# The last stage of a gated two-block transformer: extremes beside GpSimd's power, the clip factor inside the maxima's product, late products kept in PSUM, the last tokens in halves

## The chip, the cores and the metric

The kernel runs on one core of one Trainium2 chip. A core has five engines with queues of their own: TensorE (PE: matrix products into PSUM), VectorE (DVE), ScalarE (ACT), GpSimd (POOL) and SyncE (SP), which here only issues transfers between the chip's memory and SBUF. An engine works through its queue in order and waits on semaphores that other engines raise. The metric is the device time of one execution in microseconds (us); three runs of the kernel before took 977.98, 979.28 and 980.5, a median of 979.28. All times below are in us unless ns is written, and stand from the start of the profiled execution's span.

## The reference, cut to what matters

Eight batches of 256 tokens with 256 features pass four gated residual blocks: a cross attention with 16 heads, a slot router, a second cross attention with 8 heads of 128, and a feed-forward block (FFN) with simulated int8 quantization. The change is in the last of these and in the norm ahead of it:

```python
def _act_fake_quant(x, clip_factor):
    scale = jax.nn.sigmoid(clip_factor) * jnp.max(jnp.abs(x)) / QMAX
    return jnp.clip(_ste_round(x / scale), -QMAX - 1.0, QMAX) * scale
...
xq = _act_fake_quant(x, clip_x[0])
gate = jnp.einsum('bsh,ih->bsi', xq, _weight_fake_quant(w_gate))
up = jnp.einsum('bsh,ih->bsi', xq, _weight_fake_quant(w_up))
h = _act_fake_quant(jax.nn.silu(gate) * up, clip_down[0])
return jnp.einsum('bsi,hi->bsh', h, _weight_fake_quant(w_down))
...
x = x + jnp.tanh(g_ffn[1]) * _L1_ffn_ref(_layernorm(x, axis=-1), ...)
```

The two maxima run over all tokens of all batches, so nothing of the FFN can begin before the last batch's norm is known, and nothing of its second product before the largest h is known.

## The kernel before, in words

Tokens lie 128 to a tile of partitions, so a batch is two halves (t = 0, 1) of 128 x 256. All batches' x stay in SBUF (`xs`), and their normalised, transposed form for the FFN goes into `cs`.

**The second attention and what runs beside it.** `attention1` walks over 8 batches x 8 heads. For each head TensorE makes keys (L1081), scores (L1124), transposes of the exponentials (L1138) and sums (L1152); VectorE takes the scores' maxima (L1125) and ScalarE the exponentials (L1126). Every second head brings queries (L1045, moved to SBUF by VectorE at L1054), and after the eighth head the projection follows (L1165, added to x at L1179). The first attention and the router run as small pieces in between; their last pieces, of the last batches, end with `hn` (L893), `svo` (L924) and `scatter` (products L930, added to x at L932). When they are drained, at the first head of the last batch, `ffn_weights` is called: it opens the pool `fw` for the FFN's weights and, behind it, a staging pool `fs`. Both take over memory of the first block's pools, and every first use of a buffer waits for the last use of what lay there. Two staging buffers `wup` take the gate and up weights by SP's transfers (L1239, L1243) and `wdn` the down weights (L1276). VectorE reduces each to its scales (L1228) and quantizes it (L1221), ScalarE casts (L1222). The scheduler mixes these with the attention's instructions in VectorE's queue.

**The last norm.** For the last batch `norm` takes mean and variance (`ln_stats`: L251, L252), adds epsilon (L254), and GpSimd takes the power -1/2 (L255). Since the maximum of |x| after the norm follows from the extremes before it, VectorE takes maximum and minimum of each half (L1190) and puts them through the norm (L1192); the normalisation itself (L260, into `xl`) is kept back as `late`.

**The scale.** `act_scale` reduces the maxima per partition (L1467), and TensorE multiplies that column, spread over 128 columns, with the identity (L1472), which brings every partition all 128 values; VectorE takes their maximum (L1475), multiplies by the clip factor and 1/127 (L1477) and takes the reciprocal (L1479). Behind L1472, TensorE runs filler products (`keep_busy`, L1348; 8 after the first scale, 9 after the second). It is called for x, with `late` between the reduction and the product, and for h.

**The FFN.** x is quantized (L1487 on ScalarE, L1489 on VectorE), for the later batches by GpSimd's converting transfers (L1491); `expand` multiplies by the gate and up weights (L1512), ScalarE takes the silu (L1520) and partly the second factor (L1524), VectorE (L1527) or GpSimd (L1525) the product. After the scale of h it is quantized (L1581, L1582) with ScalarE and VectorE taking turns by a table, and for each batch TensorE makes two times six products of 128 x 256 into one PSUM bank (L1616). VectorE multiplies by the row of scales into `y` in SBUF (L1626), GpSimd (batches 0 to 3) or VectorE (4 to 7) adds x (L1630), SP sends the batch out (L1631). The last batch goes in two halves of tokens; in VectorE's queue both its products stand ahead of both its sums.

Of the kernel before, what the change touches and what calls it, by code (L numbers as in the profile page):

```python
# [9 lines left out]
F32 = mybir.dt.float32  # L10
# [6 lines left out]
ALU = mybir.AluOpType  # L17
AX = mybir.AxisListType
# [3 lines left out]
P = 128  # L22
B, S, D = 8, 256, 256
EPS = 1e-5
# [16 lines left out]
QMAX = 127.0  # L41
# [59 lines left out]
def flamingo_kernel(ctx: ExitStack, tc: tile.TileContext, a: dict, out: bass.AP):  # L101
    nc = tc.nc
    V, A, G, T = nc.vector, nc.scalar, nc.gpsimd, nc.tensor
# [16 lines left out]
    xs, cs = [], []  # L120
# [70 lines left out]
    ident = keep.tile([P, P], F32, tag="ident", name="ident")  # L191
# [49 lines left out]
    amax = keep.tile([P, B + 3], F32, tag="amax", name="amax")  # L241


    powers = []

    def ln_stats(src, name):

        st = small.tile([P, 2, 6], F32, tag=f"st{name}", name="st")
        mv = small.tile([P, 2, 2], F32, tag=f"mv{name}", name="mv")
        for i in range(2):  # L250
            V.bn_stats(st[:, i, :], src[:, i, :])  # L251
            V.bn_aggr(mv[:, i, :], st[:, i, :])  # L252
        rstd = small.tile([P, 2], F32, tag=f"rs{name}", name="rstd")
        V.tensor_scalar(rstd, mv[:, :, 1], EPS, None, ALU.add)  # L254
        powers.append(G.tensor_tensor(rstd, rstd, mhalf, ALU.pow).ins)  # L255
        return mv, rstd

# [747 lines left out]
    class Batch1:  # L1005
# [175 lines left out]
        def norm(self):  # L1181
            b = self.b
            self.xl = at1.tile([P, 2, D], F32, tag="tn", name="xl") if b < B - 1 else ffn["xl"]
            mv, rstd = ln_stats(xs[b], "e")
            if b == B - 1:

                ends = amax[:, b:].rearrange("p (t i) -> p t i", t=2)
                for i, op in enumerate((ALU.max, ALU.min)):
                    for t in range(2):
                        V.tensor_reduce(ends[:, t, i : i + 1], xs[b][:, t, :], AX.X, op)  # L1190
                for t in range(2):
                    V.tensor_scalar(  # L1192
                        ends[:, t, :], ends[:, t, :], mv[:, t, 0:1], rstd[:, t : t + 1], ALU.subtract, ALU.mult
                    )
                self.late = lambda: ln_apply(self.xl, xs[b], mv, rstd)
                return
            ln_apply(self.xl, xs[b], mv, rstd)
            V.tensor_reduce(amax[:, b : b + 1], self.xl, AX.XY, ALU.max, apply_absolute_value=True)
# [5 lines left out]
    def ffn_weights():  # L1204
# [129 lines left out]
            turns.append(late)  # L1334

        ffn["turns"] = [go for pair in zip(*turns[:2]) for go in pair] + turns[2]
        ffn["xl"] = fw.tile([P, 2, D], F32, tag="xl", name="xl")
        ffn.update(hq=hq, wg_s=wg_s, wu_s=wu_s, wgT=wgT, wuT=wuT, wdT=wdT, wd_row=wd_row)
        side.add([(0.7, go) for go in work])

    ffn = {}
# [111 lines left out]
    with (  # L1453
# [10 lines left out]
        def act_scale(maxima, clip_col, name, after, between=None):  # L1464

            m = fk.tile([P, 2], F32, tag=f"m{name}", name=f"m{name}")
            V.tensor_reduce(m[:, 0:1], maxima, AX.X, ALU.max, apply_absolute_value=True)  # L1467
            if between:
                between()

            pt = one()
            rows = T.matmul(pt[:, :P], m[:, 0:1].to_broadcast([P, P]), ident, start=True, stop=True)  # L1472
            with tc.issue_after(rows.ins):
                keep_busy(one(), after)
            V.tensor_reduce(m[:, 1:2], pt[:, :P], AX.X, ALU.max)  # L1475
            s = fk.tile([P, 1], F32, tag=f"s{name}", name=f"s{name}")
            V.tensor_scalar(s, m[:, 1:2], clip_col, 1.0 / QMAX, ALU.mult, ALU.mult)  # L1477
            r = fk.tile([P, 1], F32, tag=f"r{name}", name=f"r{name}")
            V.reciprocal(r, s)  # L1479
            return s, r  # L1480

        def quantize(engines, dst, src, r, name):
# [9 lines left out]
            else:  # L1492
                return (A.copy if to_bf16 == "A" else V.tensor_copy)(dst, q).ins

        sx, rx = act_scale(amax, clip[:, 0:1], "x", WARM[1], final.late)
        A.copy(cs[B - 1], turned_in(one(), final.xl))
        xqT = fk.tile([P, 2, B * S], BF16, tag="xqT", name="xqT")
# [113 lines left out]

        for b in range(B):
            pd = one().rearrange("p (t d) -> p t d", t=2)
            for t in range(2):
                for i in range(IC):
                    T.matmul(  # L1616
                        pd[:, t, :],
                        hq[:, b, i, t * P : (t + 1) * P],
                        wdT[:, i, :],
                        start=i == 0,  # L1620
                        stop=i == IC - 1,
                    )
            y = fp.tile([P, 2, D], F32, tag="y", name="y", bufs=B)
            for at in (slice(0, 2),) if b < B - 1 else (slice(0, 1), slice(1, 2)):
                n = at.stop - at.start
                V.tensor_tensor(  # L1626
                    y[:, at, :], pd[:, at, :], srow[:, None, :].to_broadcast([P, n, D]), ALU.mult
                )
                add = G if b < B // 2 else V
                add.tensor_tensor(y[:, at, :], y[:, at, :], xs[b][:, at, :], ALU.add)  # L1630
                nc.sync.dma_start(out=out_v[b][:, at, :], in_=y[:, at, :])  # L1631


# [39 lines left out]
```

## Time and profile before

| | |
|---|---|
| median of 3 runs | 979.28 (977.98 to 980.5) |
| the profiled execution | 977.07 |
| its span, from first to last instruction | 975.2, 13331 instructions, granted clock 0.996 |

How the engines' time is spread (busy time in us, share of the span, instructions):

```profile
PE 937.1 (96%) x4875; PEld 692.3 (71%) x4877; DVE 618.5 (63%) x1622; ACT 466.0 (48%) x922; POOL 139.9 (14%) x181
```

And by stretches of the end (each line: the stretch, its length, then busy time and instructions of PE, PEld, DVE, ACT, POOL, the granted clock, the DMA engines' busy share, GB/s):

```profile
880.00:919.00 39.00, 38.97 (x180) 28.86 (x179) 16.63 (x35) 16.92 (x37) 0.98 (x2) 1.00 0.00 1
919.00:928.00 9.00, 7.69 (x41) 5.06 (x39) 4.81 (x18) 0.86 (x2) 1.68 (x3) 1.00 0.00 1
...
932.00:952.00 20.00, 19.48 (x88) 8.51 (x88) 17.17 (x16) 20.00 (x36) 17.70 (x16) 1.00 0.20 35
952.00:959.00 7.00, 5.22 (x26) 2.37 (x24) 6.22 (x12) 2.00 (x4) 1.27 (x1) 1.00 0.00 0
959.00:970.00 11.00, 10.74 (x98) 9.29 (x95) 9.58 (x15) 6.89 (x5) 4.96 (x4) 1.00 0.33 112
970.00:975.20 5.20, 0.00 (x0) 0.00 (x0) 2.05 (x6) 0.00 (x0) 0.00 (x0) 0.81 0.51 172
```

The attention ends near 919, the last norm and the first scale take until 928, the expansion until 952, the second scale until 959, the last products until 970, and the last sums and transfers until 975. Filler products count as TensorE's busy time, so its busy share says little between 923 and 959.

### The profile page before, as it was taken

What the parts mean: (1) busy time and instruction counts of PE and PEld (TensorE: products, weight loads), DVE (VectorE), ACT (ScalarE), POOL (GpSimd) and SP (SyncE); (2) the same over time, 40 slices, a digit from 0 to 9 for tenths busy, and PEclk for the clock granted to TensorE, in tenths of its full rate; (3) what the DMA queues carried; (4) which work ended last, traced back from release to release, by engine and by line L of the source; (5) the groups of instructions that cost most, each with busy time, mean ns of one, the idle gap of its engine ahead of it and who ended that gap; (6) DMA issues with size and microseconds to landing.
All of it is one profiled execution on the core that took longest, in us unless ns stands there. A gap on an engine that the chain in (4) does not pass through costs nothing.

```text
span 975.2 us, 13331 instructions
## 1 busy us (share of the span) xinstructions
PE 937.1 (96%) x4875; PEld 692.3 (71%) x4877; DVE 618.5 (63%) x1622; ACT 466.0 (48%) x922; POOL 139.9 (14%) x181
## 2 busy tenths in 40 slices
PE   4989999999999999999999999999999999999996
PEld 3767778887777777777777677676667776777744
DVE  8765777774656747665657655566865365364487
ACT  3786545553546434554544443543434334333494
POOL 7101210110110202101011000013100010000172
PEclk9999999999999999999999999999999999999999
DMA  6803201111211102120001000000200000000012
GB/s 148 249 2 94 81 22 44 57 52 44 74 36 44 45 2 64 44 65 23 22 23 44 23 23 22 1 1 4 87 1 1 1 1 0 1 1 1 1 33 87
DMA packets 35186, 38.13 MB, mean 39 GB/s; under 512 B 10480, under 2 KB 30640, under 8 KB 35120
## 3 DMA queue, kind: packets, MB, share of 16 engines
q1 hardware_dynamic: 33488, 36.48, 12.8%
q0 software_dynamic: 1632, 0.79, 0.5%
q8 instruction: 39, 0.64, 0.3%
q14 instruction: 27, 0.22, 0.1%
HBM read 28.08 MB, written 8.39 MB: 37 GB/s over the span
## 4 chain that ended last, share of the span: by engine, by line
PE 82%; DVE 9%; ACT 5%; DMA 1%; issue 1%; POOL 1%; SPq 1%; DVEq 0%; ACTq 0%; POOLq 0%
PE bank_m L1152 10%; PE bank_m L1101 10%; PE bank_m L1081 10%; PE bank_m L1124 9%; PE bank_m L1045 5%; PE bank_m L1138 5%; PE bank_m L1165 5%; PE bank_z L623 3%; PE bank_z L649 2%; PE bank_z L531 2%; PE bank_z L660 2%; PE bank_s L876 1%; PE bank_z L703 1%; PE bank_z L560 1%; PE bank_z L272 1%
## 5 line engine op out<-in xcount | busy, mean ns | idle before, releaser
L1126 ACT ACTIVATE e<-bank_m,nm 128x512 f32<-128x512 f32 x128 | 88.0, 688 | 143.7 <-DVE nm L1125 141.6
L1152 PE MATMUL bank_m<-eT,v 128*128 128x256 f32 x496 | 120.6, 381 | 1.1 <-ACT k L1088 0.8
L1081 PE MATMUL bank_m<-kvT,w1kv 128*128 128x512 f32 (+1 forms) x256 | 118.4, 575 | 0.8 <-ACT e L1126 0.8
L1152 PEld LDWEIGHTS bank_m<-eT,v 128*128 128x128 f32 x496 | 92.4, 190 | 32.4 <-issue 14.8
L1101 PE MATMUL bank_m<-w1kv,kvT 128*128 128x256 f32 x480 | 110.0, 379 | 0.0
L1124 PE MATMUL bank_m<-k,q 128*128 128x512 f32 x224 | 109.5, 594 | 0.0
L1125 DVE TENSOR_REDUCE nm<-bank_m 128x1 f32<-128x512 f32 x128 | 87.6, 687 | 27.4 <-PE bank_m L1124 23.6
L1101 PEld LDWEIGHTS bank_m<-w1kv,kvT 128*128 128x128 f32 x480 | 89.8, 190 | 11.5
L652 ACT ACTIVATE e<-bank_z 128x512 f32<-128x512 f32 x112 | 62.8, 597 | 73.3 <-PE bank_z L649 72.9
L1054 DVE TENSOR_SCALAR q<-bank_m,bq 128x256 f32<-128x256 f32 x64 | 27.9, 477 | 87.3 <-PE bank_m L1045 87.3
L255 POOL TENSOR_TENSOR rstd<-rstd,mhalf 128x2 f32<-128x2 f32 x48 | 35.4, 741 | 322.7 <-DVE rstd L254 273.5
L626 DVE TENSOR_REDUCE nf<-bank_z 128x2 f32<-128x512 f32 x112 | 74.3, 681 | 9.7 <-PE bank_z L623 9.2
L1108 DVE COPY v<-bank_m 128x512 f32<-128x512 f32 x62 | 42.5, 686 | 55.2 <-PE bank_m L1101 55.2
L1138 PEld LDWEIGHTS bank_m<-ident,e 128*128 128x128 f32 x512 | 59.7, 141 | 23.6 <-issue 16.5
L1138 PE MATMUL bank_m<-ident,e 128*128 128x128 f32 x512 | 71.7, 274 | 1.3 <-DVE q L1054 1.0
L1159 ACT ACTIVATE oT<-bank_m,bv 128x256 f32<-128x256 f32 x64 | 30.3, 474 | 80.9 <-PE bank_m L1152 80.9
L1088 ACT ACTIVATE k<-bank_m,bk 128x512 f32<-128x512 f32 (+1 forms) x64 | 42.4, 662 | 47.5 <-PE bank_m L1081 47.1
L1045 PE MATMUL bank_m<-kvT,w1q 128*128 128x256 f32 x256 | 62.7, 381 | 1.7 <-DVE kvT L1035 1.4
L1128 DVE TENSOR_SCALAR e<-e,rs 128x512 f32<-128x512 f32 x128 | 62.1, 485 | 2.2
L1081 PEld LDWEIGHTS bank_m<-kvT,w1kv 128*128 128x128 f32 x256 | 43.3, 190 | 26.3 <-issue 22.1
L1165 PE MATMUL bank_m<-w1o,oT 128*128 128x256 f32 x256 | 60.1, 380 | 0.2 <-DVE x L1179 0.2
L1045 PEld LDWEIGHTS bank_m<-kvT,w1q 128*128 128x128 f32 x256 | 47.9, 190 | 11.0 <-DVE kvT L1035 2.2
(383 smaller groups left out, 1613.6 us busy)
## 6 DMA issues: line engine op xcount, KB each, us to landing
qs<-dqb SPq DMA_DIRECT2D x96, 64.0 KB, 2.6
ks<-dkb SPq DMA_DIRECT2D x48, 128.0 KB, 2.7
c<-in_ctx_dram SPq DMA_DIRECT2D x8, 256.0 KB, 3.3
x<-in_x_dram SPq DMA_DIRECT2D x8, 256.0 KB, 3.1
w1kv<-in_L_xattn_Wkv_dram SPq DMA_DIRECT2D x4, 512.0 KB, 5.4
out_dram<-y SPq DMA_DIRECT2D x7, 256.0 KB, 3.1
dqb<-hi SPq DMA_DIRECT2D x6, 256.0 KB, 2.2
dqb<-lo SPq DMA_DIRECT2D x6, 256.0 KB, 2.2
```

What stands on the lines that cost most here:

```text
L626: V.tensor_reduce(full[:, 2 * half : 2 * half + 2], ps, AX.X, ALU.max, negate=True)
L652: A.activation(e[:, i, :, :], ps, AF.Exp)
L1045: T.matmul(pq[:, i, :], w1q[:, c, h * P : (h + 1) * P], self.kvT[:, c, S:], start=c == 0, stop=c == 1,)
L1081: T.matmul(pk[:, at], w1kv[:, c, h * P : (h + 1) * P], self.kvT[:, c, at], start=c == 0, stop=c == 1,)
L1101: T.matmul(pv[:, k, :], (self.mT, self.kvT[:, :, S:])[half][:, c, k * P : (k + 1) * P], w1kv[:, c, at : at + 2 * P], start=c == 0, stop=c ...
L1124: T.matmul(ps, q, self.k[h], start=True, stop=True)
L1125: V.tensor_reduce(nm[:, at], ps, AX.X, ALU.max, negate=True)
L1126: A.activation(e[:, qc, :], ps, AF.Exp, bias=nm[:, at], accum_out=sums[:, at])
L1128: V.tensor_scalar(e[:, qc, :], e[:, qc, :], rs[:, at], None, ALU.mult)
L1138: T.transpose(pt[:, k, qc * P : (qc + 1) * P], self.e[h][:, qc, kc * P : (kc + 1) * P], ident)
L1152: T.matmul(po, self.v[h // 2][kc // 2][:, kc % 2, (h % 2) * P : (h % 2 + 1) * P], self.eT[:, kc, :], start=kc == 0, stop=kc == 3,)
L1165: self.projected = T.matmul(self.pp[:, qc, :], self.oT[:, h, qc * P : (qc + 1) * P], w1o[:, h, :], start=h == 0, stop=h == H1 - 1,).ins
```

## The change: what it does

Four edits of the last stage:

- The last norm's extremes are taken half by half, those of the second half behind the addition of epsilon in VectorE's queue, that is beside GpSimd's power; mean and reciprocal deviation are then applied to all four extremes by two operations with broadcast operands, in place of one operation for each half.
- Two diagonal matrices `dx` and `dh` (identity x clip factor / 127) are made in `ffn_weights` and kept in the pool `fw`. TensorE multiplies the maxima by them in place of the identity, and the scaling at L1477 goes. `late` is issued behind the reduction of the maxima.
- For batches 4 to 7 the product with the row of scales is written back to PSUM in place of SBUF, and the sum reads it there.
- The second half of the last batch's tokens is multiplied, scaled, added and sent in two pieces of 128 features.

```diff
-        V.tensor_scalar(rstd, mv[:, :, 1], EPS, None, ALU.add)
+        ready_for_power.append(V.tensor_scalar(rstd, mv[:, :, 1], EPS, None, ALU.add).ins)
...
-                for i, op in enumerate((ALU.max, ALU.min)):
-                    for t in range(2):
-                        V.tensor_reduce(ends[:, t, i : i + 1], xs[b][:, t, :], AX.X, op)
                 for t in range(2):
-                    V.tensor_scalar(
-                        ends[:, t, :], ends[:, t, :], mv[:, t, 0:1], rstd[:, t : t + 1], ALU.subtract, ALU.mult
-                    )
+                    with ExitStack() as late:
+                        if t:
+
+                            late.enter_context(tc.issue_after(ready_for_power[-1]))
+                        for i, op in enumerate((ALU.max, ALU.min)):
+                            V.tensor_reduce(ends[:, t, i : i + 1], xs[b][:, t, :], AX.X, op)
+                V.tensor_tensor(ends, ends, mv[:, :, 0:1].to_broadcast([P, 2, 2]), ALU.subtract)
+                V.tensor_tensor(ends, ends, rstd[:, :, None].to_broadcast([P, 2, 2]), ALU.mult)
...
+        ffn["scaled"] = {}
+        for i, name in enumerate("xh"):
+            at = ffn["scaled"][name] = fw.tile([P, P], F32, tag=f"d{name}", name=f"d{name}")
+            V.tensor_scalar(at, ident, clip[:, i : i + 1], 1.0 / QMAX, ALU.mult, ALU.mult)
         ffn["xl"] = fw.tile([P, 2, D], F32, tag="xl", name="xl")
...
-            V.tensor_reduce(m[:, 0:1], maxima, AX.X, ALU.max, apply_absolute_value=True)
+            found = V.tensor_reduce(m[:, 0:1], maxima, AX.X, ALU.max, apply_absolute_value=True).ins
             if between:
-                between()
+                with tc.issue_after(found):
+                    between()
...
-            rows = T.matmul(pt[:, :P], m[:, 0:1].to_broadcast([P, P]), ident, start=True, stop=True)
+            rows = T.matmul(pt[:, :P], m[:, 0:1].to_broadcast([P, P]), scaled[name], start=True, stop=True)
...
-            s = fk.tile([P, 1], F32, tag=f"s{name}", name=f"s{name}")
-            V.tensor_scalar(s, m[:, 1:2], clip_col, 1.0 / QMAX, ALU.mult, ALU.mult)
+            s = m[:, 1:2]
...
-            for t in range(2):
+
+            whole = [(t, slice(0, D)) for t in range(2)]
+            parts = whole if b < B - 1 else whole[:1] + [(1, slice(d, d + P)) for d in (0, P)]
+            for t, d in parts:
                 for i in range(IC):
                     T.matmul(
-                        pd[:, t, :],
+                        pd[:, t, d],
                         hq[:, b, i, t * P : (t + 1) * P],
-                        wdT[:, i, :],
+                        wdT[:, i, d],
...
-            for at in (slice(0, 2),) if b < B - 1 else (slice(0, 1), slice(1, 2)):
+            for at, d in ((slice(0, 2), slice(0, D)),) if b < B - 1 else [(slice(t, t + 1), d) for t, d in parts]:
                 n = at.stop - at.start
-                V.tensor_tensor(
-                    y[:, at, :], pd[:, at, :], srow[:, None, :].to_broadcast([P, n, D]), ALU.mult
-                )
-                add = G if b < B // 2 else V
-                add.tensor_tensor(y[:, at, :], y[:, at, :], xs[b][:, at, :], ALU.add)
-                nc.sync.dma_start(out=out_v[b][:, at, :], in_=y[:, at, :])
+                scale = srow[:, None, d].to_broadcast([P, n, d.stop - d.start])
+                add, to = (G, y) if b < B // 2 else (V, pd)
+                V.tensor_tensor(to[:, at, d], pd[:, at, d], scale, ALU.mult)
+                add.tensor_tensor(y[:, at, d], to[:, at, d], xs[b][:, at, d], ALU.add)
+                nc.sync.dma_start(out=out_v[b][:, at, d], in_=y[:, at, d])
```

More of the change, by code (lines that the diff above doesn't have):

```diff
@@ L241, in flamingo_kernel @@
     amax = keep.tile([P, B + 3], F32, tag="amax", name="amax")
-    powers = []
+    powers, ready_for_power = [], []
     def ln_stats(src, name):
@@ L1493, in quantize @@
                 return (A.copy if to_bf16 == "A" else V.tensor_copy)(dst, q).ins
+        scaled = ffn["scaled"]
         sx, rx = act_scale(amax, clip[:, 0:1], "x", WARM[1], final.late)
```

## The prediction

> **What bounds the kernel now.** I read the page's chain of work first, then the chain in order of time over the end of the run, then the waits of one window where TensorE is not full.
>
> ```profile
> PE 82%; DVE 9%; ACT 5%; DMA 1%; issue 1%; POOL 1%; SPq 1%; DVEq 0%; ACTq 0%; POOLq 0%
> ```
>
> TensorE is the bound for most of the span, so what lies beside it is free there. The edited places are three stretches in which it waits. The first is the last norm and the scale of x. Columns: start, length, what (all in us from the span's start):
>
> ```profile
> 923.56 0.48 DVE x L1179
> 924.04 0.04 DVE offset L1574
> 924.08 0.43 DVE st L251
> 924.50 0.32 DVE amax L1190
> 924.82 0.09 DVE mv L252
> 924.91 0.30 DVE amax L1190
> 925.22 0.09 DVE rstd L254
> ...
> 925.44 0.70 POOL rstd L255
> 926.14 0.03 issue
> 926.16 0.48 DVE amax L1192 x2
> 926.64 0.32 DVE xl L260
> 926.96 0.09 DVE mx L1467
> 927.04 0.14 issue
> 927.18 0.46 PE big L1472 x2
> ```
>
> Everything is serial here: two extremes stand in front of the power, one normalisation of x (L260) in front of the reduction that TensorE awaits. The second is the end, on VectorE:
>
> ```profile
> 965.85 0.69 DVE L1626 TENSOR_TENSOR y<-big,srow 128x512 f32<-128x512 f32 x1 [0.62 <-PE big L1616]
> 966.57 1.53 DVE L1630 TENSOR_TENSOR y<-y,x 128x512 f32<-128x512 f32 x1
> 968.02 0.68 DVE L1626 TENSOR_TENSOR y<-big,srow 128x512 f32<-128x512 f32 x1
> ```
>
> The sum of batch 4 takes 1.53 where the same form has a median of 0.692; a GpSimd sum of two SBUF tiles runs from 966.29 to 967.55 beside it. The products, with one operand in PSUM, run beside such GpSimd sums at 0.69. The third lies 280 us earlier, where the FFN's weights are loaded and quantized (columns: who waited for what, us in total, times, longest):
>
> ```profile
> PE bank_m L1138 <- DVE q L1054: 1.0, 1, 1.0
> ...
> DVE wu_s L1228 <- DMA wup<-in_L_ffn_w_up_dram: 0.9, 1, 0.9
> ...
> DVE wg_s L1228 <- DMA wup<-in_L_ffn_w_gate_dram: 0.5, 1, 0.5
> ...
> PE bank_m L1138 <- ACT e L1126: 0.3, 1, 0.3
> ```
>
> VectorE waits 0.5 and 0.9 for the two loads, and TensorE then waits for VectorE's late q.
>
> **The change part by part.**
>
> **W, the weights' staging, which the diff does not name.** The two new 128x128 tiles (1 KB per partition) enter the pool in front of the staging pool, whose buffers move. The changed program's list of semaphore waits shows what that does: before, the gate weights' load waited for TensorE's last use of svo (L930, 679.46 to 680.49) and was issued at 680.62, the up weights' load behind it at 681.69. Now the gate load waits only for older work, of which VectorE's L893 is the last (665.59 to 666.01), and SP has nothing else queued; the up load alone waits for L930. So gate is issued near 666.1 and lands by 671 (5.0 from issue to landing, from the list of DMA issues), up is issued near 680.6, 1.07 earlier, and lands near 685.6. VectorE, which came to its two reductions at 685.4 and would come to the second at 687.6, waits for neither: 0.53 + 0.87 = 1.40. q (L1054) starts at 692.57 instead of 693.97 and ends at 693.4. TensorE, which issues L1124's four matmuls from 692.00 on at 0.43 each, is through with them at 693.71, so its wait of 1.0 goes; the second group of L1138 at 696.29 waits for ScalarE's exponential (0.69 and its read of the sum), which follows q and L1125 on VectorE, and starts near 694.87. W = -1.4, carried to the end by TensorE-bound work. Bounds: 0 (the lead is lost again at a later wait) and -1.86, TensorE's idle time in 690 to 700 (1.32) and 700 to 710 (0.54). The two tiles themselves are two VectorE operations of 0.28 each (L1290, same form) in its 1.30 idle before L932 at 674.91; uncovered they would cost 0.5. The staging memset stays where it is in GpSimd's queue.
>
> **X, the scale of x.** With the extremes behind it, the aggregate starts at 924.55 and rstd at 924.75, not 925.13: -0.38, and the power ends at 925.75. The two extremes (0.32 each) run until 925.54 under the power. The two scalings of 0.48 become two 128x4 operations of 0.16 (L630, same form), of which the subtraction has two SBUF inputs under GpSimd's power. The nearest row: a 128x4 difference (L630) took 0.436 under a GpSimd sum and ended 0.02 after it. So it ends at 925.77, the multiplication at 925.96, and mx starts at 925.99 instead of 926.87: -0.88, of which 0.32 is the normalisation that went behind it. That one (until 926.79) is hidden by TensorE's 0.46 and the wait for it. Taking the clip factor into the matmul removes L1477 (0.25 with its gap) before the reciprocal, so ScalarE's and VectorE's first quantizations come 1.13 earlier; but TensorE has 8 filler matmuls (1.73) and four transposes behind the maxima's product, so ScalarE's copy of the last batch moves by 0.88 only. In the changed order ScalarE takes the last quantization between the first and second sg, where it idled 0.22 (931.55 to 931.77). From there ScalarE sets the pace (busy 20.00 of 932 to 952). X = -1.1; bounds -0.5 (power at its slowest row, 1.18, and no gain in the order) and -1.15.
>
> **H, the scale of h.** The same 0.25 is saved after 957.68, but the next is TensorE's queue: 9 fillers of 0.216 behind L1472, until 959.26, while the first quantized h is ready at 958.7. H = 0; without those fillers it would be -0.25.
>
> **T, the end.** Times here are in the frame of before. The sums of batches 4 to 7 read the product from PSUM, like L1626, and so are not held by GpSimd: 0.69 instead of 1.53. The product into PSUM has no row in this trace. Its bounds are 0.68 (this form into SBUF) and 1.53 (the slowest row of the form); I take 0.69, since only the destination differs. Batch 5 then starts at 967.19, when TensorE has it (967.16), batch 6 at 968.53, batch 7 at 969.86; before it was 968.02, 969.34, 970.67. The last batch's order is now product, sum, three times, in a chain: the wait lists make each further product wait for the sum before it, and the first for all 18 matmuls (TensorE's end 969.77; 12 of them at 0.057 as in L1316 against six at 0.109: +0.03). So from 969.86: 0.42 + 0.42 (the 128x256 rows), 4 x 0.28 (L687, 128x128, 0.289) and five gaps of 0.035 (as from 966.54 to 966.57) end at 972.0; before, 972.09. The last issue is at 972.03, not 972.24, where SP was still busy. In the packet records, 512-byte packets of this queue took 27 ns where 1024-byte ones take 46, eight on each DMA engine, and the new ones do not queue behind the previous transfer: data ends at 972.03 + 0.86 (issue to first packet, as before) + 0.22 = 973.11, not 973.64. T = -0.5; bounds -0.8 and +2.8 (four 128x512 equivalents at 1.53).
>
> [...]
>
> **Sum:** -1.4 - 1.1 + 0 - 0.5 = -3.0. The profiled execution took 977.07 (span 975.2 and 1.87 around it), so 974.1 in its own time. It lies 2.2 below the median of the runs, 979.28, and below their lowest; the median becomes 979.28 - 3.0 = 976.3.
>
> **Rivals.**
> - More: W takes all of TensorE's idle time there (-1.86): 975.8. For: q and nm both come earlier. Against: 0.3 of it waits for ScalarE.
> - W gives nothing, since the later of the two loads still ends the wait or VectorE's lead is lost at the next one: -1.6, 977.7. For: the title names no such part. Against: both waits are rows, and the lists show the earlier issue.
> - X is lost in the expansion, where GpSimd's six DMA issues (4.5 from 930.15) and its products set the pace: -1.9, 977.4. Against: they start behind a ScalarE quantization that moves too.
> - Slower: the product into PSUM. A write that costs as much as the slowest row of its form, 1.53, on four 128x512 equivalents that all lie on the end's chain, is 4 x 0.84 = 3.35 more than forecast: 979.6. It decides from 0.69 + 3.0 / 4 = 1.44 per product. For: no row shows such a write. Against: the row of 1.53 has its own explanation.
>
> **How the numbers follow.** Forecast 0.60, more 0.12, W nothing 0.15, X lost 0.08, slower 0.05. 0.3% is 2.94, about what a measurement of this kernel can tell from no change; it lies at 976.34, at the forecast. So some half of the forecast's chance counts as faster (0.32), with the first rival (0.12) and strays from the others (0.04) 0.48; slower by 0.3% only with a product far over 1.53 or a disturbed measurement, 0.03; the rest, 0.49, is within. Range 974.7 to 978.6: the runs before spread 2.5, the first three rivals are inside, and the slower one is left out.
>
> **What would show it.** W: gate's issue near 666, no DMA wait at L1228, no 1.0 wait of L1138 for q. X: extremes under the power, TensorE's maxima product 0.9 earlier against L1179, ScalarE's last sg 1.1 earlier. H: TensorE's L1616 still directly behind the fillers. T: every sum from PSUM at 0.69, batch 5's product at TensorE's pace, last issue 0.2 earlier. Wrong if the product into PSUM is above 0.8, if L1138 keeps its wait, or if ScalarE starts to wait in the expansion.

## The result, and the profile after

The changed kernel took 976.26 (median of 22 runs, 973.63 to 980.78), the kernel before 979.65 (22 runs, 976.19 to 981.17). The medians differ by 3.39. The ratio is 0.997, with a 95% interval of 0.9959 to 0.998, that is between 2.0 and 4.0 us less.

The two profiled executions do not show that by their times: 977.07 with a span of 975.2 before, 977.29 with one of 975.4 after. TensorE's granted clock differs between executions of one and the same kernel (a mean of 0.985 to 0.995 over the 22 of the changed one): in the first 150 us it falls to half for stretches of 3.4 us, two of them in the profiled execution before, four in the one after. Windows of the changed kernel (the stretch, its length, busy time of PE, PEld, DVE, ACT, POOL, then the granted clock, the DMA share, GB/s):

```profile
18.40:21.80 3.40, 3.40 (x8) 2.75 (x9) 1.73 (x4) 0.00 (x0) 3.40 (x5) 0.51 0.24 54
32.10:35.50 3.40, 3.40 (x11) 2.83 (x12) 0.44 (x1) 2.98 (x4) 0.23 (x1) 0.50 0.80 261
73.10:76.50 3.40, 3.40 (x23) 1.91 (x24) 1.09 (x3) 1.31 (x3) 0.00 (x0) 0.51 0.00 0
124.30:127.70 3.40, 3.40 (x11) 2.27 (x11) 2.68 (x10) 0.33 (x1) 0.00 (x0) 0.51 0.33 107
```

Nothing that the change touches lies there. So TensorE's matmuls of the two traces are paired in order here, and the difference of their starts is taken, after minus before. A number that falls from one row to the next is time gained in between:

```
us of the kernel before     shift      what lies between
140 to 693                  +2.67      two more stretches at half clock, ahead of 140
697 to 925                  +1.23      -1.44: the weights' staging
927 to 929                  +0.42      -0.81: x's maxima product
930 to 939                  +0.28      -0.14: the first quantizations
943 to 969                  +0.19      -0.09: the order on ScalarE
end of the span             +0.24      +0.05: the end
```

From 650 us on the changed kernel is 2.43 faster. The page's chain of work is what it was:

```profile
PE 82%; DVE 9%; ACT 5%; DMA 2%; issue 1%; POOL 1%; SPq 0%; ACTq 0%; DVEq 0%
```

**The middle.** The loads of the weights, from the list of the line that issues them (L1241, before L1239; duration in ns, first and last start):

```profile
L1241 SPq DMA_DIRECT2D wup<-in_L_ffn_w_gate_dram x1: 390/390/390, 668.8 to 668.8; - x1
L1241 SPq DMA_DIRECT2D wup<-in_L_ffn_w_up_dram x1: 396/396/396, 683.3 to 683.3; - x1
```

Less the 2.67 this is 666.16 and 680.62. The waits of 684 to 706 hold no line of VectorE for a load and no wait of TensorE's matmuls at L1138 for q any more. Only the weight load ahead of them (PEld) still waits for q, 0.4 where it was 1.8:

```profile
PEld bank_m L1138 <- DVE q L1054: 0.4, 1, 0.4
```

**The scale of x**, in the chain of waits (start, length, what):

```profile
924.78 0.48 DVE x L1179
...
925.98 0.17 DVE rstd L254
926.15 0.66 DVE amax L1194 x2
926.81 0.02 issue
926.83 0.17 DVE amax L1195
927.00 0.03 issue
927.03 0.02 DVEq L1196
927.05 0.04 issue
927.10 0.17 DVE amax L1196
927.27 0.02 issue
927.29 0.17 DVE mx L1474
927.47 0.14 issue
927.60 0.46 PE big L1480 x2
```

From the last L1179 to the maxima product it is 2.82 instead of 3.62. The extremes now fill the time of the power (926.29 to 926.98), and one small multiplication is left behind it.

**The end on VectorE:**

```profile
966.03 0.70 DVE L1639 TENSOR_TENSOR big<-big,srow 128x512 f32<-128x512 f32 x1 [0.62 <-PE big L1627]
966.76 0.69 DVE L1640 TENSOR_TENSOR y<-big,x 128x512 f32<-128x512 f32 x1
967.37 0.69 DVE L1639 TENSOR_TENSOR big<-big,srow 128x512 f32<-128x512 f32 x1
...
970.03 0.42 DVE L1639 TENSOR_TENSOR big<-big,srow 128x256 f32<-128x256 f32 x1
970.49 0.42 DVE L1640 TENSOR_TENSOR y<-big,x 128x256 f32<-128x256 f32 x1
970.95 0.30 DVE L1639 TENSOR_TENSOR big<-big,srow 128x128 f32<-128x128 f32 x1
...
971.94 0.29 DVE L1640 TENSOR_TENSOR y<-big,x 128x128 f32<-128x128 f32 x1
```

Batch 4's sum takes 0.69 beside GpSimd's, as was meant, and batch 5's product starts 0.83 earlier than before, counted from h's maxima product. But the last sum, counted from h's maxima product, ends at 15.19, before at 15.23: the last batch gives the lead back, in a chain of six operations in which each runs only behind the one ahead.

### The profile page after: what moved, and what is told of

Its sections match the earlier page's. It is cut to its first block, busy times and chain, and to the rows that moved or that the text cites. A ratio compares the mean times of both kernels' runs of the same rounds, so it can differ in the third digit from the quotient of the medians.

```text
span 975.4 us, 13352 instructions
## 1 busy us (share of the span) xinstructions
PE 939.2 (96%) x4883; PEld 694.6 (71%) x4883; DVE 618.8 (63%) x1624; ACT 466.3 (48%) x922; POOL 139.6 (14%) x181
## 4 chain that ended last, share of the span: by engine, by line
PE 82%; DVE 9%; ACT 5%; DMA 2%; issue 1%; POOL 1%; SPq 0%; ACTq 0%; DVEq 0%
PE bank_m L1152 10%; PE bank_m L1101 10%; PE bank_m L1081 10%; PE bank_m L1124 9%; PE bank_m L1045 5%; PE bank_m L1138 5%; PE bank_m L1165 5%; PE bank_z L623 3%; PE bank_z L649 3%; PE bank_z L531 3%; PE bank_z L660 2%; PE bank_z L703 1%; PE bank_z L560 1%; PE bank_s L876 1%; PE bank_m L272 1%
## 5 line engine op out<-in xcount | busy, mean ns | idle before, releaser
L1138 PEld LDWEIGHTS bank_m<-ident,e 128*128 128x128 f32 x512 | 59.7, 141 | 22.1 <-issue 16.5
L1138 PE MATMUL bank_m<-ident,e 128*128 128x128 f32 x512 | 71.6, 273 | 0.1
```

What stands on the lines that cost most here:

```text
L1138: T.transpose(pt[:, k, qc * P : (qc + 1) * P], self.e[h][:, qc, kc * P : (kc + 1) * P], ident)
```

## The experiments

Where stages are compared, times run from the start of h's maxima product (L1472 before, L1480 after), so that nothing ahead of it counts. "From 650 on" is the span's difference to the kernel before, less the shift of TensorE's matmuls that was already there at 600 to 650 us.

```
run                  first    last     last    end of    from     ratio to before,
                     wdT mm   sum end  issue   the span  650 on   95% interval
before               2.24     15.23    15.39   18.34      -       -
after                2.24     15.19    15.32   18.39     -2.43    0.997  (0.9959 to 0.998)
after_again          2.24     15.19    15.33   18.35     -2.49    0.998  (0.9966 to 0.9994)
tiles_alone          2.24     15.22    15.37   18.44     -1.38    1.0006 (0.9993 to 1.002)
tiles_alone_again    2.24     15.23    15.39   18.39     -1.40    0.9996 (0.9982 to 1.0009)
extremes_before      2.24     15.19    15.33   18.47     -1.74    one run
factor_apart         2.24     15.19    15.36   18.65     -1.83    one run
fill3                1.57     14.71    14.84   18.01     -2.80    one run
fill3_factor_apart   1.82     14.96    15.09   18.06     -2.46    one run
tail_before          2.24     14.99    15.13   18.19     *        0.9976 (0.9959 to 0.9993)
tail_halves          2.24     14.80    14.83   17.83     -3.01    0.9976 (0.9961 to 0.9992)
products_first       2.24     14.28    14.43   17.48     -3.37    0.9986 (0.9966 to 1.0006)
combined             1.59     13.79    14.25   18.22     -2.62    0.997  (0.9949 to 0.999)
two_queues           1.59     13.80    13.83   17.35     -3.51    0.9983 (0.9968 to 0.9997)
```

(* its profile has a stretch at half clock at 690 us.) The medians depend on the granted clock: over all kernels that were timed more than once, a line with one slope for all of them gives 0.63 us for each 0.001 of mean clock (0.984 to 0.996 occur), and leaves 0.8 us of scatter. Where a time "at the same clock" is given, it is from that line, as the difference to the kernel before, with a 95% interval. By it the kernels with another end stand at -2.54 (the old end), -2.66 (halves) and -2.31 (products first), 0.50 either way each, and the changed kernel at -2.78 (0.39): the times do not tell these ends apart, and what is said of them rests on one profile each.

**The staging alone.** Two tiles, made and never read, in the kernel before:

```diff
+        for i, name in enumerate("xh"):
+            at = fw.tile([P, P], F32, tag=f"d{name}", name=f"d{name}")
+            V.tensor_scalar(at, ident, clip[:, i : i + 1], 1.0 / QMAX, ALU.mult, ALU.mult)
         ffn["xl"] = fw.tile([P, 2, D], F32, tag="xl", name="xl")
```

> The kernel before with nothing but the two 128x128 tiles made (and never read), in the pool ahead of the staging pool. If the staging explains the gain in the middle: the gate weights' load is issued some 14.5 us earlier than before relative to TensorE's L930 work, VectorE's two waits for the loads (0.53 and 0.87) are gone, TensorE's 1.0 wait of L1138 for q is gone, and every TensorE instruction from 697 us on stands 1.4 us earlier against those of 650 us than in the kernel before; the time falls by 1.4 us (ratio 0.9985) at the same granted clock. If the middle gains from something else of the change, or the lead is lost again: no shift after 697 us, ratio 1.000. The tail is that of before: 18.34 us from h's maxima product to the end of the span.

Measured: TensorE's matmuls stand at +2.48 against the kernel before until 690 and at +1.03 from 700 on: -1.45. The gate load of this kernel and one window of TensorE, first of the kernel before:

```profile
690.00:700.00 10.00, 8.68 (x36) 5.55 (x35) 9.51 (x28) 5.97 (x16) 0.00 (x0) 1.00 0.00 1
```

and of this one, 2.5 later by its own start:

```profile
L1239 SPq DMA_DIRECT2D wup<-in_L_ffn_w_gate_dram x1: 389/389/389, 668.6 to 668.6; - x1
```

```profile
692.50:702.50 10.00, 9.90 (x42) 6.90 (x42) 9.29 (x27) 6.79 (x19) 0.00 (x0) 1.00 0.00 0
```

TensorE is busy for 9.90 of the ten instead of 8.68. The whole gain in the middle thus comes with the two tiles, and nothing of the last stage is needed for it. That it is the staging buffers' new place, and not the two extra VectorE operations, is read from the gate load: it is issued 14.5 earlier against TensorE, as the list of semaphore waits had it. No run moves the buffers without the operations. The median did not follow (980.01 against 979.29), at a mean clock of 0.9899 against 0.9915. So I ran it again:

> The kernel before with nothing but the two unused tiles, once more. Its profile showed the shift of 1.44 in full, its median did not (979.29 before, 980.01 with the tiles, at mean granted clocks of 0.9915 and 0.9899). If the clock is what hid it, the time at the same granted clock is again lower by about 1, and the mean clock is no longer lower than that of the kernel before; rival, the tiles themselves lower the granted clock (by 0.0015 or more again), so that the median gains nothing.

The profile shows the same -1.43 step. The median is now 979.1 against 980.03, at mean clocks of 0.9903 and 0.9908. At the same clock the two give -0.59 (0.50 either way) and -1.00 (0.50): the sign is that of the traces, the size lies below their 1.4, outside the interval the first time and inside it the second. Twelve runs do not settle half a microsecond here. That the tiles lower the clock is not borne out by the second set.

**The two parts of x's scale**, each undone in the changed kernel. First the extremes:

```diff
-                for t in range(2):
-                    with ExitStack() as late:
...
-                V.tensor_tensor(ends, ends, mv[:, :, 0:1].to_broadcast([P, 2, 2]), ALU.subtract)
-                V.tensor_tensor(ends, ends, rstd[:, :, None].to_broadcast([P, 2, 2]), ALU.mult)
+                for i, op in enumerate((ALU.max, ALU.min)):
+                    for t in range(2):
+                        V.tensor_reduce(ends[:, t, i : i + 1], xs[b][:, t, :], AX.X, op)
+                for t in range(2):
+                    V.tensor_scalar(
+                        ends[:, t, :], ends[:, t, :], mv[:, t, 0:1], rstd[:, t : t + 1], ALU.subtract, ALU.mult
+                    )
```

> The changed kernel with the extremes of x's last batch taken and scaled as in the kernel before (all four reductions in one loop, one scaling of two columns for each half of the tokens); the normalisation stays behind the maximum and the clip factor stays in the product. By the prediction the extremes in front of the power and the two dearer scalings cost 0.88 - 0.32 = 0.56, and the normalisation the 0.32: so from the last L1179 to x's maxima product 3.3 us here, against 2.82 in the changed kernel and 3.62 before, and everything behind it 0.5 later. Rival, it is the order behind the maximum alone that gained (or the subtraction is held by GpSimd's power so that nothing is won under it): 2.8 to 2.9, no shift.

Measured: 3.43 (3.3 expected), and all behind it 0.61 later than in the changed kernel (0.5 expected), up to the last sum. The timeline of VectorE in this run (in brackets the idle time ahead, and whom it waited for):

```profile
927.44 0.16 DVE L254 TENSOR_SCALAR rstd<-mv 128x2 f32<-128x2 f32 x1
928.47 0.48 DVE L1192 TENSOR_SCALAR amax<-amax,mv,rstd 128x2 f32<-128x2 f32 x2 [0.87 <-POOL rstd L255]
```

VectorE stands idle for 0.87 under the power and takes its two scalings of 0.48 behind it: this is the part that gained. Then the clip factor:

```diff
-            rows = T.matmul(pt[:, :P], m[:, 0:1].to_broadcast([P, P]), scaled[name], start=True, stop=True)
+            rows = T.matmul(pt[:, :P], m[:, 0:1].to_broadcast([P, P]), ident, start=True, stop=True)
...
-            s = m[:, 1:2]
+            s = fk.tile([P, 1], F32, tag=f"s{name}", name=f"s{name}")
+            V.tensor_scalar(s, m[:, 1:2], clip_col, 1.0 / QMAX, ALU.mult, ALU.mult)
```

> The changed kernel with the clip factor applied by an instruction of its own again, before both reciprocals; the two scaled tiles are still made. By the prediction: from the reduction behind x's maxima product to the first quantization 0.78 instead of 0.52, and 0.24 longer from x's maxima product to h's (29.68 instead of 29.44, as before); for h the same 0.25 is hidden behind nine fillers, L1627 starts directly behind them, and 18.2 to 18.4 remain from h's maxima product to the end. Rival, the order of ScalarE's work gained the 0.24: 29.44 here too. Rival for h: the end shifts by 0.25 as well.

Measured: the first quantization 1.36 instead of 1.11 behind x's maxima product, and 29.77 from x's product to h's, against 29.44 in the changed kernel and 29.68 before. The factor is worth 0.33 on this stretch, more than the 0.24 expected. The one instruction is 0.25 of it. The other 0.08 is ScalarE's order: in this run it takes its last quantization behind the second sg, as before, and stands idle for 0.24 ahead of that sg; in the changed kernel the quantization fills this gap. Without the factor the rest of the change even costs 0.09 here (29.77 against 29.68; the reason is given below). For h, L1627 starts at 2.24 in both, and the last sum ends at 15.19 in both.

**Without the cover.** In the changed kernel, and in the one with the factor apart, `WARM = (12, 8, 15, 9)` became `(12, 8, 15, 3)`:

> The changed kernel with 3 instead of 9 fillers behind h's maxima product. If the fillers cover the wait for the first quantized h: L1627 starts when the first quantized part is ready, some 1.5 us after the product's start instead of 2.24, and the end comes 0.6 to 0.7 earlier (17.7 us from h's maxima product against 18.39). Rival, the quantizations or VectorE's tail set the end, or TensorE's clock falls without the fillers: the end moves by less than 0.2 or comes later.

> As the run with 3 fillers, with the clip factor as an instruction of its own. The prediction says that without the fillers h's shorter chain is worth 0.25: L1627 starts 0.25 later after h's maxima product than with 3 fillers alone, and the end is 0.25 later. Rival, the chain of h is hidden by something else too: no difference.

Measured: 1.57 and 1.82; the last sum ends at 14.71 and 14.96. The chains of waits, with 3 fillers alone, and with the factor apart:

```profile
955.98 0.30 DVE mh L1483
956.28 0.02 issue
956.30 0.17 DVE rh L1486
956.48 0.02 issue
956.50 0.50 DVE hq L1590
957.00 0.05 issue
957.05 0.39 PE big L1627 x2
```

```profile
959.64 0.30 DVE mh L1483
959.94 0.02 issue
959.97 0.23 DVE sh L1485
960.19 0.02 issue
960.22 0.17 DVE rh L1487
```

The one instruction is 0.25, and it counts in full once fewer fillers lie in front. The ends of the two spans differ by 0.05 only, and not by the 0.25 expected, since what follows the last sum differs: 3.30 to the end of the span in one, 3.10 in the other. With three fillers TensorE starts 0.67 earlier and then loses 0.18 waiting for quantized h: 0.48 is left at the last sum, and 0.38 at the end, less than the 0.6 to 0.7 expected.

**The end.** Three variants of the changed kernel. Undone as a whole (the lines of the kernel before, products into y, two halves):

> The changed kernel with the end of the kernel before (products into y, last batch in two halves). The prediction as recorded: the new end is worth 0.5, so this kernel is 0.5 us slower than the changed one and takes 18.9 us from h's maxima product to the end of the span. Rival, from the changed kernel's trace (18.39 against 18.34 before): the new end is worth nothing as a whole, so this one takes 18.34 and its time is that of the changed kernel within 0.1. Batch 4's sum should again take 1.5 beside GpSimd's, and the last four operations 1.42 us together, not 2.20.

With two halves, still product and sum in one PSUM tile:

```diff
-            parts = whole if b < B - 1 else whole[:1] + [(1, slice(d, d + P)) for d in (0, P)]
+            parts = whole
```

> The changed kernel with the last batch in two halves of 256 columns instead of one half and two quarters, still in one PSUM tile. If the chain of product, sum, product, sum (each waits for the one before: 0.46 from start to start of 128x256) is what eats the gain: four steps, 1.80 us from the last batch's first product to its last sum, not 2.20, last issue 0.4 earlier; the last transfer is twice as long (some 0.2), so the end is 0.2 earlier, 18.2 us from h's maxima product. Rival, the finer split pays by its shorter last transfer: the end is the same or up to 0.2 later than the changed kernel's, 18.4 to 18.6.

And, also in two halves, with one PSUM tile for each half and both products ahead of the sums:

```diff
-            pd = one().rearrange("p (t d) -> p t d", t=2)
+            pds = [one().rearrange("p (t d) -> p t d", t=2) for _ in range(1 if b < B - 1 else 2)] * 2
...
+            for at, d in split:
+                V.tensor_tensor((y if to is y else pd)[:, at, d], pd[:, at, d], scale, ALU.mult)
+            for at, d in split:
+                add.tensor_tensor(y[:, at, d], (y if to is y else pd)[:, at, d], xs[b][:, at, d], ALU.add)
```

> The changed kernel with the last batch's two halves in two PSUM tiles and both products ahead of the sums. If the chain in one PSUM tile eats the gain: the first half's product waits only for its own six matmuls and is done between batch 6's product and sum, the other half's product and the two sums overlap (0.335 from start to start), the last sum ends 0.78 earlier than in the changed kernel, and the end comes 0.6 earlier: 17.8 us from h's maxima product. Rival, the end is set by SP's issues and the transfers and not by VectorE: the last sum is earlier but the end by less than 0.2, 18.2 or more.

Measured: 18.19, 17.83 and 17.48, against 18.39 in the changed kernel. Both expectations for the old end were off: within the changed kernel it is 0.2 *faster* than the new one. Batch 4's sum shows why (VectorE's timeline with the old end):

```profile
971.64 1.29 DVE L1639 TENSOR_TENSOR y<-y,x 128x512 f32<-128x512 f32 x1
```

It takes 1.29, not 1.53, and the last sum ends at 14.99, 0.20 before that of the new end. GpSimd's four sums start 0.25 earlier against h's maxima product (the last at 9.18, before at 9.43), since VectorE got to the first products 0.24 earlier, and so the sum beside them, 1.53 before, is through earlier. This is h's 0.25, which does not show on TensorE. The chain is confirmed: in two halves it takes, from the last batch's first product to the end of its last sum, 1.81 (1.80 expected) instead of 2.20; the end came 0.56 earlier than in the changed kernel, where 0.2 was expected. With two tiles VectorE reads:

```profile
970.24 1.04 DVE L1639 TENSOR_TENSOR big<-big,srow 128x512 f32<-128x512 f32 x2
971.19 0.68 DVE L1642 TENSOR_TENSOR y<-big,x 128x512 f32<-128x512 f32 x1
971.79 0.42 DVE L1639 TENSOR_TENSOR big<-big,srow 128x256 f32<-128x256 f32 x1
972.12 0.74 DVE L1642 TENSOR_TENSOR y<-big,x 128x256 f32<-128x256 f32 x2
```

The first half's product is taken together with batch 6's (x2), the last product and the two sums overlap, and the last sum ends 0.92 earlier than in the changed kernel, 0.78 being expected. Of this 0.39 comes with the halves (14.80), and 0.52 with the two tiles and the order together; no run separates these two.

**Both, and where it stuck.** Two tiles and 6 fillers:

> The changed kernel with the last batch's halves in two PSUM tiles, both products ahead of the sums, and 6 instead of 9 fillers behind h's maxima product. If the two gains add up (0.91 from the first and some 0.5 from fewer fillers, by the two runs apart): L1627's first matmul 1.6 us after h's maxima product, the last sum's end at 13.8, the end at 17.0 us after it, against 18.39 in the changed kernel; at the same granted clock the time is 1.4 us below the changed kernel's. Rival, with TensorE earlier the quantized h or GpSimd's sums of the first four batches become late and the tail keeps VectorE at 17.4.

Measured: the last sum ends at 13.79, as expected, but the span at 18.22, 1.2 later than expected. The rival named VectorE's tail as the reason; it was not that, since VectorE was through in time. SP's issues (shortest, median and longest in ns):

```profile
L1643 SPq DMA_DIRECT2D out_dram<-y x9: 372/438/1545, 960.9 to 968.4; - x9
```

Batch 4's sum is ready at 964.04, but its issue stands behind that of batch 3, whose GpSimd sum ends at 964.58; then it takes 1.55, and the next four follow close on one another until 968.98. In the packet records a packet of 16 KB on an instruction queue is under way from 964.5 to 966.2. Letting ScalarE issue three of the outputs:

```diff
-                nc.sync.dma_start(out=out_v[b][:, at, d], in_=y[:, at, d])
+                (nc.scalar if b in (4, 5) or (b == 7 and at.start == 0) else nc.sync).dma_start(out=out_v[b][:, at, d], in_=y[:, at, d])
```

> The combined kernel with the outputs of batches 4 and 5 and of the last batch's first half issued by ScalarE, whose own work is over by then, and the others by SP. If SP's queue is what held the combined kernel (batch 4's output behind batch 3's, one issue of 1.55 instead of 0.37, the last issue 0.45 behind the last sum): batch 4's output is issued within 0.2 of its sum, the last issue 0.15 behind the last sum, at 13.95 from h's maxima product, and the end comes at 17.0 to 17.3, not 18.2; at the same granted clock the time is 1 us below the combined kernel's and 1.2 below the changed kernel's. Rival, the transfers themselves are held (packets of the instruction queue on one DMA engine, 2 MB at some 340 GB/s): the last packet again lands 16.2 or later, the end at 17.9 or later.

Measured: the last issue at 13.83, the end at 17.35, just outside the 17.0 to 17.3 expected.

```profile
L1643 SPq DMA_DIRECT2D out_dram<-y x6: 351/373/384, 965.4 to 972.5; - x6
L1643 ACTq DMA_DIRECT2D out_dram<-y x3: 351/378/421, 968.6 to 972.1; - x3
```

No issue is held, and by the trace this is the fastest of all from 650 us on: 3.51 less than before, 1.02 to 1.08 less than the two profiles of the changed kernel. The times do not show it: 976.64 at a mean clock of 0.9905, and at the same clock -2.83 (0.50 either way), where the changed kernel has -2.78 (0.39) and the combined one -3.06 (0.56). The 1 us and 1.2 us that were expected against these two are missed. No version is therefore shown by its times to beat the changed kernel; that this one does rests on one profile. The gain over the combined kernel has two possible causes, too. In the other thirteen profiles the last 16 KB packet of an instruction queue starts 10.4 to 11.4 behind h's maxima product and takes 0.88 to 1.73, while outputs are under way; in this one, with three issues fewer on SP, it starts at 19.0, behind the end. No run tells the second issuer from the missing packet.

**The changed kernel again:**

> The changed kernel itself once more, beside the others on one chip. If the sum of the traces is right (-1.44 in the middle, -1.05 at x, nothing at the end) its time is 2.4 to 2.5 us below that of the kernel before at the same granted clock. In the end the last transfer, though half as long as before, again needs 1.36 us or more from its issue to its last packet, since a packet of the instruction queue holds one DMA engine; rival, that was an accident of one profile: 1.1.

Measured: 978.45 against 980.03, at mean clocks of 0.9892 and 0.9908; at the same clock -2.44 (0.50), with -2.49 in the trace, as expected. The last packet again comes 1.36 after its issue; that an instruction packet holds a DMA engine is my reading of it and is not shown, since the records name no engine.

## Why the prediction was right, and where it was not

The time was forecast as 976.3 and came to 976.26. That the two agree so closely is partly luck. The forecast's 3.0 less was 2.4 to 2.5 in the traces and 2.78 (0.39) at the same clock; the medians differ by 3.39, and the kernel before came to 979.65 in 22 runs, 0.37 above the 979.28 that the forecast started from. Of its three terms that are not zero two held, and the third, T, came to nothing.

- **W, -1.4: right in every step that the traces show.** Gate's issue 666.16 (forecast 666.1), up's 680.62 (680.6), no wait for a load at L1230 (before L1228), no 1.0 wait for q, q at 692.53 (692.57), the second group of L1138 at 694.85 (694.87); -1.44 kept to the end. The runs with the tiles alone show that the two tiles are the whole cause. The rivals (1.86, nothing) fell.
- **X, -1.1: measured -1.04 to -1.05.** The maxima product came 0.81 earlier, not 0.88; the first quantization 0.97 earlier, not 1.13. Two things were mis-sized.

  The first is the multiplication behind the power. The subtraction ended when forecast (927.00, or 925.77 in the frame of before), though for another reason: it was not held by the power, but started behind the second pair of extremes and took its usual 0.16. The multiplication, however, started 0.10 behind it, with a wait on VectorE's queue in between (L1196 at 927.03), and not 0.03; so it comes 0.07 later.

  The second is the normalisations. Of the two that moved behind the maximum, the second starts at 927.88 and lets the reduction L1483 follow only at 928.20, 0.60 behind the maxima product, where it was 0.49 before. The forecast called them hidden; 0.1 of them is not. The run with the factor apart shows the same 0.09, from 29.68 to 29.77. They can be hidden: in the run with the extremes undone they start 0.23 ahead of the maxima product, the reduction comes at 0.50 and the first quantization at 1.02. In the changed kernel they start only 0.06 ahead of it; why, no run tells.

  In the expansion 0.09 was won by ScalarE's order, where the forecast had counted on 0.22 of its idle time. The rival that loses X in the expansion fell: TensorE's lead still grows there, its shift going from +0.28 to +0.19. (The bound of -0.5 should have read -0.4: 0.88 less the 0.48 of the slowest power. Nothing here hangs on it.)
- **H, 0: right for TensorE, incomplete for the rest.** L1627 starts directly behind the nine fillers, and without them the 0.25 appears, as said. Not seen: VectorE and GpSimd get it in spite of the fillers, and with the old end it is worth 0.24 at batch 4's sum.
- **T, -0.5: this step failed.** Together with H it gave +0.05 in the first profile, nothing within 0.1 over those with this end (18.35, 18.39 and 18.47, against 18.34, 18.39 and 18.44 in the three of the old kernel). At the last sum the two can be told apart: without H the new end is worth 0.04 (15.23 before, 15.19 with the factor apart), and with H it costs 0.20 (14.99 with the old end, 15.19 with the new one), since the old end takes H's 0.24 and the new one does not. (With the factor apart the span ends at 18.65; the 0.26 over the changed kernel came behind the last sum, in one profile, and is no price of T.)

  Its parts: the product into PSUM, the unknown, took 0.69 to 0.70, as chosen, so the slower rival fell; the last sum ended 0.04 earlier, where 0.09 was forecast. The issue was put 0.03 behind the sum; it came 0.13 behind it, as it did before (0.155), a row that I had put down to a busy SP.

  The last transfer, half as long, was to be through 1.08 after its issue; it needed 1.36, no less than the 1.38 of the one twice its size. In the packet records a packet of 8 KB on an instruction queue runs from 15.96 to 16.50 (counted from h's maxima product). All but eight packets of output are through by 16.51, that is 1.19 behind the issue, 0.11 over the forecast; the last eight follow one by one until 16.68. Eight is one DMA engine's share of this transfer, if its 128 packets of 512 bytes are spread evenly over 16 engines, so it looks as if the instruction packet held one engine; the records do not name it. All six profiles with a 64 KB last transfer show such a packet 0.6 to 0.8 behind the last issue; in those with 128 KB it comes 1.4 or more behind, when the data is through or nearly so. This is so in every profile, but no run moves the packet. And 0.13 more came behind the data: from the last packet to the end of the span it was 1.57 before and 1.70 after.

The larger finding is one that the forecast had in its sum but did not follow up: it counted the chain and put the last sum only 0.09 earlier, though a contention of 0.84 was gone. The same edit removed the contention and tied the last six operations into a chain that gave it back. Products first, in two tiles, keep the gain in the one profile of that kernel: its last sum ends 0.95 earlier than in the kernel before, H's 0.24 included.

What the two tiles change shows in the start of the last batch's first product: in the eleven profiles with one tile it never starts before TensorE's last matmul is done (12.99 against 12.89 in the changed kernel), and in the three with two tiles it starts 0.62 before that (12.26 against 12.88 with products first). That the shared tile is what it waits for is not shown, since with one tile batch 6's sum also stands ahead of it on VectorE. In this chain a wait for the result costs: an independent 128x256 operation follows 0.33 after the start of the one ahead (products first), one that needs its result 0.46 after it (two halves in one tile).

## What to carry to other kernels

Read a change's effect on buffer addresses as well as its named edits: a new small tile that moves a staging pool can be worth more than the rest (here 1.44 of 2.43). When an operation is made cheaper at the end of a kernel, look at what it is chained to and what the last issue and transfer wait for, before the saving is booked; here independent 128x256 operations overlapped (0.33 from start to start, at 0.42 each) and dependent ones did not (0.46). And when the granted clock moves single runs by several microseconds (here 973.63 at 0.995 and 980.78 at 0.985), compare traces by the shift of paired instructions, stage by stage.

## What the runs showed of the hardware

- TensorE's clock fell to half in stretches of 3.41 us, 2 to 8 of them before 150 us in the fourteen profiles, and different numbers in two profiles of one kernel (4 and 6 in the changed one): mean clocks of 0.985 to 0.996, and 0.63 us for each 0.001.
- VectorE writing into PSUM (128x512, float32, the other operand from SBUF): 0.69 to 0.70, against 0.68 to 0.69 into SBUF; 128x256 0.42 to 0.43, against 0.41 to 0.42. Reading one operand from PSUM, 128x512, with the result in SBUF: 0.69 in the kernel before (L1626) and in the changed one (L1640), where the sum of two SBUF tiles takes 0.69 as well (L1630, two of three; the third is that of 1.53).
- SP's issue of a 256 KB output takes 0.37, but in twelve of the fourteen profiles the fifth or sixth of the nine or ten takes 0.60 to 1.55 (in the combined kernel the last one 0.62 as well). In eleven of the twelve that issue starts while a 16 KB packet on an instruction queue is under way, in the twelfth 0.02 behind it, and it ends 0.2 to 0.8 behind the packet's end. The run with two queues has no such packet there and no long issue; in the other, the second one of the tiles alone, no issue starts during the packet. It looks as if the issue waits for the packet, but no run moves the packet on its own.
- At the kernel's end, packets on the instruction queues take 0.36 to 0.60 (8 KB) and 0.88 to 1.73 (16 KB). With three of the nine outputs issued by ScalarE, between the combined kernel and the one with two queues the end came 0.87 earlier, in one profile each, with the 16 KB packet gone as well.
